# Reciprocal square root of the last three sequences' final layernorm: one GpSimd power, or a Newton iteration on VectorE

## The chip, the cores and the metric

The kernel runs on one core of a Trainium2 chip. A core has five engines that work side by side, each through its own instruction queue in the order in which it was written: TensorE (PE, with its weight loads PEld), VectorE (DVE), ScalarE (ACT), GpSimd (POOL) and SyncE (SP, which here only issues transfers). They wait for each other by semaphores. The metric is the device time of one execution in microseconds (us); a measurement is the median of several executions.

## The reference, cut to what matters

One layer over 16 sequences of 512 tokens with 128 features, all in float32: an attention block with a gate and a layernorm, then a mixture of 8 experts plus a shared expert. After each of the two blocks the sum with its input is normalized:

```python
def _layernorm(x, axis=-1, eps=1e-05):
    m = jnp.mean(x, axis=axis, keepdims=True)
    v = jnp.var(x, axis=axis, keepdims=True)
    return (x - m) / jnp.sqrt(v + eps)
...
    x = L0_attn_x
    x = _layernorm(x + _L0_attn_ref(x, ...), axis=-1)
    x = _layernorm(x + _L0_ffn_ref(x, ...), axis=-1)
    return x
```

In `_L0_ffn_ref` the part that ends last here is the shared expert, `silu(x @ sg) * (x @ su) @ sd` with 1024 hidden features. The kernel adds it to the routed experts' output and to the input, and the second `_layernorm` then gives the result. The change concerns only the `1 / sqrt(v + eps)` of that second layernorm, and of it only the last three of the 16 sequences.

## The kernel before, in words

The 8192 tokens are 64 tiles of 128 tokens (one token to a partition); a sequence is `NC = 4` tiles and there are `NT = 64` tiles. The kernel has two phases. The first does the attention, the first layernorm and the routing; the second does the routed experts and then a closing loop. Work of the shared expert is cut into small steps and kept in a list, `feed`, from which both phases take steps to fill TensorE.

The order of instructions on PE, DVE, ACT and POOL is exactly the order in which Python writes them (`manual_schedule`, no planner). So an instruction that waits holds up everything behind it on its engine.

What the change and its surroundings touch:

- `shared_steps` (the shared expert of one sequence). Eight "gate" steps (`pg`, L125, then ACT's Silu `sl`, L127) alternate with eight "up" steps (`pu`, L133, then DVE's product `h`, L134). Then come eight "down" steps: for each of the sequence's four tiles two halves of the product with `sd` (`pd`, L143), and behind the second half DVE adds the tile's input rows and so empties the accumulator (`x1T<-pd,x`, L148).
- `shared_order` puts the down steps of a sequence behind the first four gate and up steps of the next; the last sequence's down steps have nothing behind them.
- Buffers that bind these steps: three PSUM buffers each for `pg` and `pu` (pool `ps_g`), two for `pd` (pool `ps_d`), two SBUF buffers for `sl`, four for each small tile of the layernorm (pool `small`).
- `finish_lot` (the second layernorm). A lot is a whole sequence (4 tiles) for the first 15 sequences, and a single tile for the four tiles of the last one. For each lot it computes, per tile, the statistics (`st`, L101, and mean and variance `mv`, L103, both DVE), then the reciprocal root by `rstd_of`: DVE adds eps (`ve`, L107), and POOL raises that to the power -0.5 (`rstd`, L109). Then DVE forms `nb = -mean * rstd` (L906), ACT writes `res = rstd * x + nb` for each tile (L909), and SP sends `res` out (L914).
- The closing loop (the `while feed or ends:` at the end of the kernel) takes a step of `feed`, then, once the routed rows are summed, lets `finish_lot` go on to its next `yield`. Two yields lie between `rstd_of` and `nb`, so other DVE work may be written between them while `feed` lasts.

`rstd_of` is used by the first phase also (function `after`, lines 509 and 524); these uses are the same in both kernels.

Of the kernel before, what the change touches and what calls it, by code (L numbers as in the profile page):

```python
# [10 lines left out]
F32 = mybir.dt.float32  # L11
I32 = mybir.dt.int32
AF = mybir.ActivationFunctionType
ALU = mybir.AluOpType
# [5 lines left out]
P = 128  # L20
B, N, D = 16, 512, 128
NC = N // P
T = B * N
NT = T // P
# [5 lines left out]
LN_EPS = 1e-5  # L30
# [17 lines left out]
def tile_kernel(  # L48
# [20 lines left out]
    nc = tc.nc  # L69
# [4 lines left out]
    small = ctx.enter_context(tc.tile_pool(name="small", bufs=4))  # L74
# [23 lines left out]
    def ln_stats(src, mv, n):  # L98
        st = small.tile([P, n, 6], F32, tag="st", name="st")
        for c in range(n):  # L100
            nc.vector.bn_stats(st[:, c, :], src[:, c, :])  # L101
        for c in range(n):
            nc.vector.bn_aggr(mv[:, c, :], st[:, c, :])  # L103

    def rstd_of(var, n, eps):
        ve = small.tile([P, n], F32, tag="ve", name="ve")
        nc.vector.tensor_scalar(ve, var, eps, None, ALU.add)  # L107
        r = small.tile([P, n], F32, tag="rstd", name="rstd")
        nc.gpsimd.tensor_tensor(r, ve, neghalf[:, :n], ALU.pow)  # L109
        return r  # L110


# [64 lines left out]
    with ExitStack() as ph:  # L177
# [317 lines left out]
        def after(b):  # L495
# [11 lines left out]
            mv = small.tile([P, NC, 2], F32, tag="mv", name="mv")  # L507
            ln_stats(o, mv, NC)
            r = rstd_of(mv[:, :, 1], NC, LN_EPS)
            yield  # L510
            w = wk1.tile([P, NC, D], F32, tag="w", name=f"w_{b}")
# [10 lines left out]
            mv2 = small.tile([P, NC, 2], F32, tag="mv2", name="mv2")  # L522
            ln_stats(w, mv2, NC)
            r2 = rstd_of(mv2[:, :, 1], NC, LN_EPS)
            yield
            yield
# [209 lines left out]
        with tc.manual_schedule(engines=ORDERED):  # L736
# [42 lines left out]
            t, over = NT + 1, 12  # L779
# [16 lines left out]
    with ExitStack() as ph:  # L796
# [96 lines left out]
        def finish_lot(lot):  # L893

            n = lot[1] - lot[0]
            mv = small.tile([P, n, 2], F32, tag="mv", name="mv")
            for t in range(*lot):
                while t not in done or t // NC not in summed:
                    yield False
                ln_stats(base[:, t : t + 1, :], mv[:, t - lot[0] : t - lot[0] + 1, :], 1)  # L900
                yield True
            rs = rstd_of(mv[:, :, 1], n, LN_EPS)
            yield True
            yield True
            nb = small.tile([P, n], F32, tag="nb", name="nb")
            nc.vector.scalar_tensor_tensor(nb, mv[:, :, 0], -1.0, rs, ALU.mult, ALU.mult)  # L906
            res = fp.tile([P, n, D], F32, tag="res", name=f"res_{lot[0]}")
            for c in range(n):
                nc.scalar.activation(  # L909
                    res[:, c, :], base[:, lot[0] + c, :], AF.Identity, bias=nb[:, c : c + 1], scale=rs[:, c : c + 1]  # L910
                )
                if c < n - 1:
                    yield True
            nc.sync.dma_start(outv[:, lot[0] : lot[1], :], res)  # L914
            yield True
# [4 lines left out]
        with tc.manual_schedule(engines=ORDERED):  # L920
# [27 lines left out]

            adds = [add_up(b) for b in range(B)]
            ends = [finish_lot(lot) for lot in lots]  # L950
            begun, landed = 0, None

# [72 lines left out]
```

## Time and profile before

| what | value |
|---|---|
| median of 3 runs | 923.22 us (922.89 to 923.61) |
| profiled execution, device time | 925.82 us |
| profiled execution, span from first to last instruction | 924.1 us |
| PE busy | 851.1 us, 92% of the span |
| DVE busy | 557.6 us, 60%, 1687 instructions |
| ACT busy | 442.7 us, 48% |
| POOL busy | 346.7 us, 38%, 461 instructions |
| POOL power, L109, of a 4-tile lot | median of all 51: 1019 ns; in the last sequences 1.01 us |
| POOL power, L109, of a 1-tile lot | 0.54 to 0.55 us, 4 of them |
| last matmul ends | at 910.79 us |
| last ACT instruction starts | at 915.19 us |

Times in the profile are microseconds from the start of the span. A row of the timeline gives the start, the duration, the engine, the line, the operation and the tiles (written `out<-in`), and in brackets the engine's idle time before it with what ended it. An instruction may start before the one ahead of it on its engine has ended, where it doesn't read that one's result: so start-to-start distances, not durations, tell what a chain of instructions takes.

### The profile page before, as it was taken

To read this page: it belongs to the slowest core of one execution; us is meant where nothing else is said; L and a number is where in the kernel's file an instruction comes from. 1 tells how busy PE (TensorE), PEld (TensorE's weight loads), DVE (VectorE), ACT (ScalarE), POOL (GpSimd) and SP (SyncE) were. 2 spreads that over 40 slices of the span, in tenths; PEclk is the share of its full clock that TensorE was granted. 3 is DMA by queue.
4 is the path that set the end of the run, shared out by engine and by line. 5 is a ranking of instruction groups with operands and counts; after the bars stand their busy time and mean duration, and the time that the engine had idled before them with its cause. 6 is when DMAs were issued, how large, how long until landed. Compare 5 with 4: busy or idle time off the path is not lost.

```text
span 924.1 us, 24551 instructions
## 1 busy us (share of the span) xinstructions
PE 851.1 (92%) x9790; PEld 582.2 (63%) x9790; DVE 557.6 (60%) x1687; ACT 442.7 (48%) x1285; POOL 346.7 (38%) x461
## 2 busy tenths in 40 slices
PE   2898999989898898888899999999999999999994
PEld 1666667656765675565555576667777666666663
DVE  6688888976589687778652433333333248854542
ACT  3767677656576665654332233333333324334341
POOL 4022222176733667666656233333333311010100
PEclk9999999999999999999899999999999999999997
DMA  9931111111111111000000522133311035501000
GB/s 279 416 143 32 31 32 31 31 43 57 46 43 34 43 59 50 24 17 9 6 2 2 151 78 64 58 90 87 92 46 37 26 106 171 159 23 35 23 24 23
DMA packets 64339, 62.97 MB, mean 68 GB/s; under 512 B 6179, under 2 KB 55130, under 8 KB 63200
## 3 DMA queue, kind: packets, MB, share of 16 engines
q1 hardware_dynamic: 57392, 50.44, 17.4%
q0 software_dynamic: 6656, 10.69, 3.6%
q8 instruction: 77, 1.26, 0.6%
q14 instruction: 38, 0.31, 0.1%
q10 hardware_dynamic: 176, 0.27, 0.1%
HBM read 32.71 MB, written 31.88 MB: 70 GB/s over the span
## 4 chain that ended last, share of the span: by engine, by line
PE 79%; DVE 13%; issue 3%; ACT 3%; DMA 1%; POOL 0%; POOLq 0%; DVEq 0%; ACTq 0%
PE pd L143 12%; PE pg L125 11%; PE pu L133 10%; PE ped L852 8%; PE peg L936 7%; PE peu L938 7%; PE pe L444 4%; PE pq L363 4%; DVE et L451 3%; PE pout L486 3%; PE pt L399 2%; PE pout L477 2%; PE po L501 1%; PE pout L468 1%; PE pq L366 1%
## 5 line engine op out<-in xcount | busy, mean ns | idle before, releaser
L671 POOL DMA_INDIRECT xg_dram<-x,idx x128 | 134.1, 1048 | 40.3 <-issue 34.4
L109 POOL TENSOR_TENSOR rstd<-ve,neghalf 128x4 f32<-128x4 f32 (+1 forms) x51 | 52.9, 1038 | 250.9 <-DVE ve L107 237.5
L451 DVE TENSOR_TENSOR et<-pe,causal 128x384 f32<-128x384 f32 x256 | 125.0, 548 | 20.4 <-PE pe L444 19.1
L858 POOL DMA_INDIRECT y_dram<-y,to x80 | 77.6, 970 | 153.6 <-ACT y L856 153.6
L941 DVE TENSOR_TENSOR eh<-esl,peu 128x512 f32<-128x512 f32 (+1 forms) x96 | 57.5, 599 | 127.7 <-PE peu L938 125.5
L125 PE MATMUL pg<-x1T,sg_sb 128*128 128x512 f32 x256 | 133.6, 604 | 0.9 <-DVE x1T L148 0.9
L134 DVE TENSOR_TENSOR h<-sl,pu 128x512 f32<-128x512 f32 x128 | 87.7, 685 | 74.5 <-PE pu L133 57.6
L133 PE MATMUL pu<-x1T,su_sb 128*128 128x512 f32 x256 | 131.7, 596 | 0.6 <-DVE h L134 0.3
L127 ACT ACTIVATE sl<-pg 128x512 f32<-128x512 f32 x128 | 76.1, 596 | 111.8 <-PE pg L125 85.8
L143 PEld LDWEIGHTS pd<-sd_sb,h 128*128 128x128 f32 x1024 | 122.9, 197 | 6.7 <-issue 5.5
L143 PE MATMUL pd<-sd_sb,h 128*128 128x128 f32 x1024 | 126.3, 280 | 0.4 <-ACT sl L127 0.4
L852 PEld LDWEIGHTS ped<-rd,eh 128*128 128x128 f32 x640 | 83.9, 192 | 23.7 <-issue 21.8
L936 PE MATMUL peg<-xgT,rg 128*128 128x512 f32 (+1 forms) x192 | 84.6, 522 | 0.0
L938 PE MATMUL peu<-xgT,ru 128*128 128x512 f32 (+1 forms) x192 | 84.4, 521 | 0.0
L852 PE MATMUL ped<-rd,eh 128*128 128x128 f32 x640 | 84.3, 275 | 0.0
L940 ACT ACTIVATE esl<-peg 128x512 f32<-128x512 f32 (+1 forms) x96 | 50.5, 526 | 59.1 <-PE peg L936 49.9
L133 PEld LDWEIGHTS pu<-x1T,su_sb 128*128 128x128 f32 x256 | 45.8, 191 | 46.4 <-issue 40.2
L856 ACT ACTIVATE y<-ped,wt 128x128 f32<-128x128 f32 x80 | 29.4, 368 | 86.8 <-PE ped L852 82.2
L363 PE MATMUL pq<-W,xT 128*128 128x384 f32 x128 | 62.8, 575 | 7.4 <-DVE W L335 6.5
L125 PEld LDWEIGHTS pg<-x1T,sg_sb 128*128 128x128 f32 x256 | 44.9, 193 | 39.0 <-issue 33.7
L486 PE MATMUL pout<-et,vpad 128*32 128x64 f32 x2048 | 50.5, 221 | 13.7 <-issue 13.7
L444 PE MATMUL pe<-q,kT 32*64 32x192 f32 x2048 | 62.1, 338 | 0.0
(165 smaller groups left out, 1285.8 us busy)
## 6 DMA issues: line engine op xcount, KB each, us to landing
y_dram<-zero SPq DMA_DIRECT2D x8, 1024.0 KB, 14.4
y<-y_dram SPq DMA_DIRECT2D x32, 256.0 KB, 3.0
xT<-xt SPq DMA_DIRECT2D x16, 384.0 KB
xg_dram<-empty SPq DMA_DIRECT2D x8, 660.0 KB, 14.6
xg<-xg_dram SPq DMA_DIRECT2D x8, 660.0 KB
x<-x SPq DMA_DIRECT2D x16, 256.0 KB, 2.9
o<-res SPq DMA_DIRECT2D x15, 256.0 KB, 2.3
xg_dram<-x,idx POOLq DMA_INDIRECT x128
```

Source lines behind the costliest of these rows:

```text
L125: nc.tensor.matmul(pg, sg_sb[:, ts(i, P)], seq, start=True, stop=True)
L133: nc.tensor.matmul(pu, su_sb[:, ts(i, P)], seq, start=True, stop=True)
L134: nc.vector.tensor_tensor(h[i // half][:, i % half, :], h.pop(("s", i)), pu, ALU.mult)
L143: nc.tensor.matmul(pd, h[k][:, i - k * half, ts(c, P)], sd_sb[:, i, :], start=(i == 0), stop=(i == IS // P - 1))
L363: nc.tensor.matmul(pq[:, :, 0:24], xts[b][:, c, 0:P], W[:, 0:384].rearrange("p (h n) -> p h n", n=24), start=True, stop=True)
L444: nc.tensor.matmul(pes[g][mine, s], kT[rows, s, mine], q2[rows, s, 3 * i : 3 * i + 3], start=(s == 0), stop=(s == 1),)
L451: nc.vector.tensor_tensor(et.rearrange("p s k n -> p s (k n)"), pes[g].rearrange("p s k n -> p s (k n)"), causal.rearrange("p k n -> p (k ...
L486: nc.tensor.matmul(pout[32 * a : 32 * a + 32, HALF:], vp[:, at : at + 32], et[g][:, s, 1 + j, :], start=False, stop=(gg == 1 and j == 1),)
L671: i = nc.gpsimd.indirect_dma_start(out=xg_dram[:, :], out_offset=bass.IndirectOffsetOnAxis(ap=idx[:, k, t : t + 1], axis=0), in_=x1[:, t, ...
L852: nc.tensor.matmul(pd, h[:, i, ts(c, P)], got[e][2][:, i, :], start=(i == 0), stop=(i == IR // P - 1))
L936: nc.tensor.matmul(pg[:, :n], rg_sb[:, ts(i, P)], xgTs[e][:, ds(o0, n)], start=True, stop=True)
L938: nc.tensor.matmul(pu[:, :n], ru_sb[:, ts(i, P)], xgTs[e][:, ds(o0, n)], start=True, stop=True)
```

## The change: four Newton steps on VectorE

A second way to compute the reciprocal root, `rstd_by_steps`, is added. It adds eps as before, makes a first guess from the bits of the number (shift right by one as an integer, subtract from a constant), and improves it by four Newton steps of three instructions each, `r <- r * (1.5 - 0.5 * ve * r * r)`. All are DVE instructions on a tile of 128 partitions with one element for each tile of the lot. `finish_lot` uses it where the lot starts at tile 52 or later: the two 4-tile lots of sequences 13 and 14, and the four 1-tile lots of sequence 15. All other lots, and the first phase, keep the power on POOL.

```diff
@@ rstd_of (before: L104 to L110) @@
         nc.gpsimd.tensor_tensor(r, ve, neghalf[:, :n], ALU.pow)
+        return r
+
+    def rstd_by_steps(var, n, eps):
+
+        ve = small.tile([P, n], F32, tag="ve", name="ve")
+        nc.vector.tensor_scalar(ve, var, eps, None, ALU.add)
+        guess = small.tile([P, n], I32, tag="guess", name="guess")
+        nc.vector.tensor_scalar(guess, ve.bitcast(I32), 1, None, ALU.arith_shift_right)
+        nc.vector.tensor_scalar(guess, guess, -1.0, float(0x5F3759DF), ALU.mult, ALU.add)
+        r = guess.bitcast(F32)
+        for step in range(4):
+            t = small.tile([P, n], F32, tag="newton", name="newton")
+            nc.vector.tensor_tensor(t, r, r, ALU.mult)
+            nc.vector.scalar_tensor_tensor(t, t, -0.5, ve, ALU.mult, ALU.mult)
+            to = small.tile([P, n], F32, tag="rstd", name="rstd")
+            nc.vector.scalar_tensor_tensor(to, t, 1.5, r, ALU.add, ALU.mult)
+            r = to
         return r
@@ finish_lot @@
-            rs = rstd_of(mv[:, :, 1], n, LN_EPS)
+
+            rs = (rstd_by_steps if lot[0] >= NT - 3 * NC else rstd_of)(mv[:, :, 1], n, LN_EPS)
```

## The prediction

> **What bounds the kernel now.** I read the page first, then the chain of waits of the last 20 us, then the timeline of that stretch, and last the timeline for rows that price a chain of tiny VectorE instructions. The page gives the whole (span, and the group that the change replaces in part):
>
> ```profile
> span 924.1 us, 24551 instructions
> L109 POOL TENSOR_TENSOR rstd<-ve,neghalf 128x4 f32<-128x4 f32 (+1 forms) x51 | 52.9, 1038 | 250.9 <-DVE ve L107 237.5
> ```
>
> POOL is idle before these powers (250.9 us in all, waiting for `ve`): it has nothing else to do. What matters is who waits behind. The chain of waits, in order of time, shows that TensorE carries it without a gap to 910.79 and that behind it stands a serial tail:
>
> ```profile
> 886.18 7.14 PE pd L143 x64
> 893.33 0.86 PE pg L125 x2
> ...
> 903.63 7.16 PE pd L143 x64
> 910.79 0.02 issue
> 910.81 0.29 DVE x1T L148
> ...
> 915.19 0.49 ACT res L909
> ```
>
> Until 903.63 a longer wait on DVE or ACT costs time only if it reaches a TensorE buffer. Of the tail, the timeline shows (start, duration, engine, line):
>
> ```profile
> 906.32 0.15 DVE L107 TENSOR_SCALAR ve<-mv 128x1 f32<-128x1 f32 x1
> 907.24 0.29 DVE L148 TENSOR_TENSOR x1T<-pd,x 128x128 f32<-128x128 f32 x1 [0.76 <-PE pd L143]
> ...
> 911.02 0.14 DVE L107 TENSOR_SCALAR ve<-mv 128x1 f32<-128x1 f32 x1
> 911.33 0.55 POOL L109 TENSOR_TENSOR rstd<-ve,neghalf 128x1 f32<-128x1 f32 x1 [4.13 <-DVE ve L107]
> 911.92 0.16 DVE L906 SCALAR_TENSOR_TENSOR nb<-mv,rstd 128x1 f32<-128x1 f32 x1 [0.76 <-POOL rstd L109]
> 912.00 0.29 DVE L101 BATCH_NORM_STATS2 st<-x1T 128x6 f32<-128x128 f32 x1
> ...
> 912.53 0.15 DVE L107 TENSOR_SCALAR ve<-mv 128x1 f32<-128x1 f32 x1
> ...
> 914.94 0.16 DVE L906 SCALAR_TENSOR_TENSOR nb<-mv,rstd 128x1 f32<-128x1 f32 x1 [0.75 <-POOL rstd L109]
> ```
>
> When TensorE ends, three 1-tile lots (tiles 61, 62, 63) are still to be normalized, one after the other: the statistics of a lot are written behind `nb` of the one before. `ve` to `nb` takes 911.92 - 911.02 = 0.90 us, and 914.94 - 914.04 = 0.90 for the last; from `ve` to the next `ve` is 1.51. So 3 x 0.90 = 2.7 us of the tail are the trip to POOL and back. That is all that the change can gain there, and it holds only if its own instructions cost less.
>
> **The price of a step.** At the start of the kernel there is a chain of instructions on 128x1 tiles, integer ones among them, each reading the one ahead, and one that doesn't:
>
> ```profile
> 2.13 0.15 DVE L238 TENSOR_SCALAR rowi<-rowi 128x1 int32<-128x1 int32 x1
> 2.32 0.15 DVE L240 CAST bitf<-rowi 128x1 f32<-128x1 int32 x1
> 2.50 0.15 DVE L242 TENSOR_SCALAR par<-bitf 128x1 f32<-128x1 f32 x1
> 2.58 0.14 DVE L243 TENSOR_SCALAR par<-bitf 128x1 f32<-128x1 f32 x1
> ```
>
> Dependent instructions start 0.19 and 0.18 apart, that is a duration of 0.15 plus some 0.035; the independent pair starts 0.08 apart. With four columns, line 539 to 541 (453.96, 454.15, 454.35) gives 0.19 and 0.20. `nb`, the scalar-tensor-tensor form that eight of the new instructions have, lasts 0.156 on 128x1, 6 ns more than `ve`. I take 0.187 a step for one column and 0.195 for four. The shift and the integer subtraction aren't in the trace: lower bound 0.08 (the independent pair), upper 0.25 (the 128x4 integer cast at 1.34); over three lots that is -0.6 to +0.4 us. I take 0.187, since line 238 is an integer instruction of the same size.
>
> **Part by part.**
>
> 1. The last three lots. Each loses the trip to POOL (0.90) and gets `ve`, two for the guess and 4 x 3 for the steps, 15 dependent instructions: 15 x 0.187 = 2.81. Each is 1.91 longer, nothing lies beside it, and all three stand in series: 3 x 1.91 = **+5.73 us**.
>
> 2. The lot of tile 60 falls between TensorE's last tiles. Today `ve` starts at 906.32, the power runs on POOL, and meanwhile DVE empties the accumulator of tile 61 at 907.24. In the changed order the 14 new instructions stand ahead of that: the last starts at 906.32 + 14 x 0.187 = 908.94, tile 61 is emptied from 909.02 to 909.31. There are two `pd` buffers, so tile 63's down step needs the one of tile 61. It would have started at 903.63 + 3 x 1.79 = 909.00 and now starts at 909.36 (TensorE followed a release by 0.05 at 14.21); 0.19 more if the first weight load is no longer hidden. So TensorE stalls 0.36 to 0.55; I take **+0.45 us**, all on the path.
>
> 3. Sequence 13's lot (4 tiles). `ve` at 885.72, last step at 885.72 + 14 x 0.195 = 888.45. Behind it wait on DVE the product `h` (888.53 instead of 886.29), `nb` (889.14) and the emptying of tile 56's accumulator (889.22 to 889.51 instead of 888.01). TensorE needs that buffer for the third tile at 886.18 + 3.57 = 889.75. **Zero**, with 0.24 us to spare; without the cover, 14 steps that are 10 ns longer each cost 0.14. The ACT work that waits for `nb` has until 894.29, ACT's next Silu.
>
> 4. Sequence 14's lot. `ve` at 895.76, last step 898.49; `h` of up step 3 ends at 899.26, `nb` 899.18, first `res` 899.37, and queued behind it on ACT is the Silu of gate step 4 (899.77 instead of 898.07). Its `h` ends at 901.08; TensorE needs that `pu` buffer for up step 7 at 902.77. The Silus catch up (901.14, 902.03, and 902.81 as today), and the last `h` starts at 903.74 as today. **Zero**, 1.7 us to spare.
>
> 5. The added waits. The four results of a lot use up the four `rstd` buffers, so the fourth waits for ACT's `res` of the lot before. That one ends 0.74 us after its `nb`, some 2.5 us ahead of need: zero. POOL loses six powers with nothing behind them, and SP's sends are later as their lots are: zero. What follows the last ACT instruction (915.68 to 924.1) is taken as it is.
>
> **Sum**: 5.73 + 0.45 = +6.18 us. The profiled execution took 925.82 (924.1 and 1.7 around the span), 2.6 over the median of the runs; I set the sum on the median: 923.22 + 6.18 = **929.4 us**, and expect a span of some 930.3 in a like profile.
>
> [...] The trace shows a toll that hardly depends on size: 0.15 us for one column, 0.29 for 128. [...]
>
> **Rivals.**
>
> - Not slower: the steps overlap on DVE as the independent pair does, 0.08 apart. Then `ve` to `nb` is 14 x 0.08 + 0.187 = 1.31, the three lots add 3 x 0.41 = 1.2, and item 2 goes: 924.4, within 0.2%. The whole decides at 0.90 / 15 = 0.06 a step, where nothing is lost. Against it: every new instruction reads its predecessor's result, and such pairs stand 0.18 to 0.20 apart in each place I found. 3%.
> - The end isn't set by the last `res`: 8.4 us of the span lie behind it without any engine at work. If something else fixes the end, 6 us could vanish there: 923.2. Against it: the chain of waits ends with that `res`, and its transfer can only follow. 2%.
> - The 4-tile lots stall TensorE too: item 3 has 0.24 us. At 0.21 a step the lots give 6.8, item 2 some 0.8, item 3 a little: 930.9. 5%.
> - Steps as slow as line 540's multiplication at 66.94, 0.44 instead of 0.16 at 454.15. Twelve such a lot would be 2.6 more a lot: over 937. Against it: POOL's addition on line 433 ran at the same moment, and in the last 20 us POOL would be empty. 1%.
> - The switch doesn't reach these lots: it compares the lot's first tile with 52, and in the built kernel's order DVE has 84 instructions more (6 x 14) and POOL six fewer. 1%.
>
> **How the numbers follow.** The forecast holds 88%. Its own ends: at 0.18 a step 5.4 + 0.27, 928.9; at 0.205 a step 6.5 + 0.8, 930.5; the integer instructions move the low end to 928.3, and the runs' own spread is 0.4. The range, 928.0 to 930.8, leaves out the first two rivals, the slow steps and some of the third. A change of 0.2%, 1.85 us, is what a measurement of this kernel can tell from none: slower 0.94 (forecast, stalls, slow steps), same 0.05 (overlap, end not set by the tail), and 0.01 for faster, the last rival's share with room for a gain that I see no case for.
>
> **What would show it.** DVE 1771 instructions, POOL 455; `ve` to `nb` 2.8 us in the last lots with the steps 0.19 apart; a TensorE gap of about half a us ahead of the last tile's down step and none earlier than 903; the same 8.4 us behind the last `res`. I am wrong if steps stand 0.1 apart, if TensorE waits at 889 or 899, or if the stretch behind the last `res` shrinks.

## The result, and the profile after

| | before | changed |
|---|---|---|
| median of 22 executions each | 924.05 us | 925.12 us |
| ratio | 1 | 1.0007 (95%: 0.9994 to 1.002) |
| profiled span | 924.1 us | 923.5 us |

No difference that this measurement can tell; the forecast was +6.2 us. The profile shows the 6.2 us, and where as much was given back. In the changed kernel the lines behind the new `rstd_by_steps` are shifted by 17, and from its call in `finish_lot` on by 18: `ve` is L115, the guess L117 and L118, the steps L122 to L125, `x1T` L165, `pd` L160, `nb` L924, `res` L927; the kernel's closing code, L1021 before, is L1039.

First the chain that ended last, of the changed kernel (start, duration, engine, tile, line):

```profile
901.94 1.80 PE pd L160 x16
...
907.75 2.07 PE pd L160 x16
909.84 0.29 DVE x1T L165
...
920.13 0.17 DVE nb L924
920.38 0.49 ACT res L927
```

From the emptying of the last accumulator to the last `res` it is 920.38 - 909.84 = 10.54 us; before it was 915.19 - 910.81 = 4.38. The tail grew by 6.16 us. Its timeline shows why, for tile 61:

```profile
910.05 0.14 DVE L115 TENSOR_SCALAR ve<-mv 128x1 f32<-128x1 f32 x1
910.22 0.15 DVE L117 TENSOR_SCALAR guess<-ve 128x1 int32<-128x1 int32 x1
910.41 0.15 DVE L118 TENSOR_SCALAR guess<-guess 128x1 int32<-128x1 int32 x1
910.60 0.16 DVE L122 TENSOR_TENSOR newton<-guess 128x1 f32<-128x1 f32 x1
...
912.53 0.16 DVE L123 SCALAR_TENSOR_TENSOR newton<-newton,ve 128x1 f32<-128x1 f32 x1
912.80 0.16 DVE L125 SCALAR_TENSOR_TENSOR rstd<-newton,rstd 128x1 f32<-128x1 f32 x1
912.99 0.16 DVE L924 SCALAR_TENSOR_TENSOR nb<-mv,rstd 128x1 f32<-128x1 f32 x1
913.07 0.28 DVE L101 BATCH_NORM_STATS2 st<-x1T 128x6 f32<-128x128 f32 x1
...
913.61 0.15 DVE L115 TENSOR_SCALAR ve<-mv 128x1 f32<-128x1 f32 x1
```

The steps start 0.19 apart, the integer ones too; only the last one of each of these three lots starts 0.27 behind its predecessor (it waits for ScalarE also, as the last section shows). `ve` to `nb` is 2.94 us where it was 0.90, and a lot takes 3.56 where it took 1.51. TensorE too stalls ahead of the last tile's down step, as these rows of its timeline (weight loads, then matmuls) say in the brackets:

```profile
907.75 1.86 PEld L160 LDWEIGHTS pd<-sd_sb,h 128*128 128x128 f32 x16 [0.64 <-DVE x1T L165]
907.75 2.05 PE L160 MATMUL pd<-sd_sb,h 128*128 128x128 f32 x16 [0.45 <-DVE x1T L165]
```

What gave it back stands behind the last `res`. The rows of the closing code's line list instructions that aren't counted as work: number, durations in ns (least, median, most), first and last start in us. Before:

```profile
L1021 POOLq DRAIN  x3: 40/102/8990, 914.3 to 923.8; - x3
L1021 SPq DRAIN  x3: 7/7/7, 917.4 to 923.6; - x3
L1021 POOLq EVENT_SEMAPHORE_RANGE_CLEAR  x1: 138/138/138, 923.7 to 923.7; - x1
```

After:

```profile
L1039 POOLq DRAIN  x3: 40/102/9455, 875.1 to 923.2; - x3
L1039 SPq DRAIN  x3: 7/7/7, 922.6 to 922.9; - x3
L1039 POOLq EVENT_SEMAPHORE_RANGE_CLEAR  x1: 137/137/137, 923.0 to 923.0; - x1
```

GpSimd's last power, before and after:

```profile
914.37 0.54 POOL L109 TENSOR_TENSOR rstd<-ve,neghalf 128x1 f32<-128x1 f32 x1 [0.97 <-DVE ve L107]
```

```profile
875.14 1.01 POOL L109 TENSOR_TENSOR rstd<-ve,neghalf 128x4 f32<-128x4 f32 x1 [9.03 <-DVE ve L107]
```

At its end each engine here has a drain, an instruction of the closing code that isn't counted as work (the closing line has such rows for all five queues), and in both kernels the end came behind all of them. SP was ready at 917.4 before: the last transfer, issued at 915.7, had landed (a 64 KB `res` took a median of 1.5 us to land). GpSimd wasn't. Its queue began to drain at 914.34, just as its last power started, and the drain lasted 8.99 us, to 923.33, which is 8.42 us behind the end of that power (914.91). Only then did the engines' last instructions follow, from 923.4 on; this meeting of the engines is the rest, 0.78 us. In the changed kernel GpSimd's last power is that of sequence 12, the drain begins at 875.1 and ends 8.42 us behind that power, at 884.57, beside other work. Then SP is the last to be ready, at 922.6, and the span ends 2.58 us behind the last `res` instead of 8.43.

So the change takes 5.85 us off behind the last `res` and puts 6.16 us and the stall ahead of it. Over the stretch from the last matmul to the end the two nearly cancel: 13.66 us after, 13.33 before. That two amounts with separate causes came out so alike is chance.

### The profile page after: what moved, and what is told of

Read it like the earlier page. It is cut to its first block, busy times and chain, and to the rows that moved or that the text cites. A ratio compares the mean times of both kernels' runs of the same rounds, so it can differ in the third digit from the quotient of the medians.

```text
span 923.5 us, 24626 instructions
## 1 busy us (share of the span) xinstructions
PE 847.2 (92%) x9790; PEld 580.0 (63%) x9790; DVE 571.3 (62%) x1771; ACT 442.3 (48%) x1285; POOL 342.7 (37%) x455
## 4 chain that ended last, share of the span: by engine, by line
PE 77%; DVE 15%; issue 4%; ACT 3%; DMA 1%; DVEq 0%; ACTq 0%
PE pd L160 11%; PE pg L142 10%; PE pu L150 10%; PE ped L869 8%; PE peg L954 7%; PE peu L956 7%; PE pe L461 4%; PE pq L380 4%; DVE et L468 4%; PE pout L503 3%; PE pt L416 2%; PE pout L494 2%; PE po L518 1%; PE pq L383 1%; DVE st L101 1%
## 5 line engine op out<-in xcount | busy, mean ns | idle before, releaser
L688 POOL DMA_INDIRECT xg_dram<-x,idx x128 | 134.1, 1048 | 40.2 <-issue 34.5
L109 POOL TENSOR_TENSOR rstd<-ve,neghalf 128x4 f32<-128x4 f32 x45 | 48.8, 1083 | 216.4 <-DVE ve L107 202.2
L160 PE MATMUL pd<-sd_sb,h 128*128 128x128 f32 x1024 | 126.9, 281 | 2.1 <-issue 1.2
L160 PEld LDWEIGHTS pd<-sd_sb,h 128*128 128x128 f32 x1024 | 123.1, 197 | 8.2 <-issue 6.3
```

What stands on the lines that cost most here:

```text
L160: nc.tensor.matmul(pd, h[k][:, i - k * half, ts(c, P)], sd_sb[:, i, :], start=(i == 0), stop=(i == IS // P - 1))
L688: i = nc.gpsimd.indirect_dma_start(out=xg_dram[:, :], out_offset=bass.IndirectOffsetOnAxis(ap=idx[:, k, t : t + 1], axis=0), in_=x1[:, t, ...
```

## The experiments

Two explanations were put against each other. Theory A: the closing drain of GpSimd, 8.42 us behind its last instruction, set the end before, and the change moves it out of the way. Theory B: the stretch behind the last `res` shrank because something counted from TensorE's end fixes the end; both kernels end 13.3 to 13.7 us behind the last matmul. Theory C, where it appears, is the forecast's own assumption that the stretch behind the last `res` is constant. The experiments ran on other chips than the result, where the kernel before takes 888 to 889 us; each ratio is against the kernel before on the same chip. The first half of the kernel varies by some 2 us from one execution to the next: on one chip the same down steps of the middle start at 461.62 in the profile of the changed kernel and at 463.82 in that of the run with one lot and steps, though the two differ only at their end. So the stretch from the last matmul to the end of the span is the sharper number, and the time the confirmation.

**A late instruction on GpSimd.** Both kernels add to the changed one, behind the `rs = ...` line of `finish_lot`:

```diff
+            if lot[0] == NT - 1:
+                late = small.tile([P, n], F32, tag="late", name="late")
+                nc.gpsimd.tensor_tensor(late, mv[:, :, 1], neghalf[:, :n], ALU.pow)   # or ALU.mult
```

> The changed kernel with one more power on GpSimd, on the variance of tile 63 into a tile that nobody reads; all lots keep their Newton steps. Theory A (the closing drain): GpSimd's drain ends 8.42 us after its last power, and the span 0.78 us after the later of this drain and the last output's landing. The power can start some 0.25 us behind mv of tile 63 (7.3 us behind the last matmul) and lasts 0.55, so the span should end 7.6 + 0.55 + 8.42 + 0.78 = 17.3 us behind the last matmul instead of 13.6, and the kernel take 3.7 us more than the changed one. Theory B (the stretch behind the last res is set by something else, counted from TensorE's end): 13.3 to 13.6 us behind the last matmul, no change of time.

> As the run with the late power, but a multiplication in its place. If the long drain follows any GpSimd arithmetic: the span ends some 16.9 us behind the last matmul (the multiplication is 0.2 to 0.55 us) and the kernel takes 3.3 to 3.7 us more than the changed one. If it belongs to the power alone: drain under 1 us, 13.6 us behind the last matmul, no change. Theory B: no change.

Measured behind the last matmul: 17.18 us with the power, 16.82 with the multiplication (0.19 us long). Against the kernel before: 1.005 (1.0033 to 1.0067), that is +4.4 us, and 1.0071 (1.0056 to 1.0085), +6.3 us. Theory A asked for some 0.7 + 3.7 = 4.4 and 4.1; the multiplication's run is 2 us over that, which its profile doesn't show; the two runs' intervals overlap, and I leave it open. The rows of the power's run, GpSimd's timeline and the closing line, and the closing line of the multiplication's:

```profile
883.00 0.55 POOL L923 TENSOR_TENSOR late<-mv,neghalf 128x1 f32<-128x1 f32 x1 [41.07 <-DVE mv L103]
```

```profile
L1042 POOLq DRAIN  x3: 40/102/9007, 883.0 to 892.5; - x3
```

```profile
L1042 POOLq DRAIN  x3: 40/102/8647, 882.8 to 892.0; - x3
```

The drain ends 8.42 us behind the late instruction in both. An instruction on GpSimd whose result nobody reads moves the end, from 13.66 us behind the last matmul in the changed kernel to 17.18 and 16.82; theory B falls, and that the instruction is a power has no part in it.

**The changed kernel with less of a chain, and once more.**

```diff
-        for step in range(4):
+        for step in range(3):
```

> The changed kernel with three Newton steps instead of four. Theory A: in the changed kernel the chain on VectorE sets the end, since the drain is long over; three instructions of 0.193 us less in each of the last three lots are 1.75 us, and TensorE's stall of 0.45 us ahead of the last tile goes: 2.2 us less than the changed kernel, 1.4 less than the kernel before; 11.9 us from the last matmul to the end. Theory B: 13.3 to 13.6 us behind the last matmul, only the 0.45 us of the stall is saved.

> The changed kernel itself, for a price on the same chip as the next three. Theory A: the tail behind the last matmul is 13.66 us (before 13.33) and TensorE stalls 0.45 us ahead of the last tile: 0.8 us over the kernel before. Theory C (the forecast on record: the stretch behind the last res is fixed): 6.2 over.

The shorter one: 11.84 us behind the last matmul, as theory A said; in time 0.9996 (0.9986 to 1.0005), that is -0.4 us with the expected -1.4 just outside the interval's end of -1.2. The changed kernel on another chip: 13.66 us behind the last matmul again, 1.0008 (0.9996 to 1.0021), where theory C wanted 6.2 us. With the drain hidden, the chain on VectorE does set the end. The steps cost about what the forecast said, but more stands against them than the 0.90 us a lot: the drain too.

**Steps for the last two lots alone.**

```diff
-            rs = (rstd_by_steps if lot[0] >= NT - 3 * NC else rstd_of)(mv[:, :, 1], n, LN_EPS)
+            rs = (rstd_by_steps if lot[0] >= NT - 2 else rstd_of)(mv[:, :, 1], n, LN_EPS)
```

> The Newton steps only for the lots of tiles 62 and 63; all others keep the power. Theory A: the last power is that of tile 61, it ends 1.1 us behind the last matmul, its drain with the 0.78 behind it 10.3 us behind the last matmul; the chain of the two lots, each 2.04 us longer, ends with the output's landing 11.6 us behind it. The later of the two, 11.6, is 1.8 us less than the kernel before (13.3). Theory C: two lots of 2.04 more, 4.1 us over the kernel before.

11.69 us behind the last matmul, and 0.9982 (0.9968 to 0.9995), -1.6 us. The closing line:

```profile
L1039 POOLq DRAIN  x3: 40/102/9002, 873.2 to 884.1; - x3
L1039 SPq DRAIN  x3: 7/7/7, 883.5 to 883.8; - x3
```

The long drain ends at 873.17 + 9.00 = 882.17, ahead of SP at 883.5. So moving GpSimd's last power forward by two lots is enough to hide the drain, and the chain is shorter by one lot's steps.

**One lot for tiles 61 to 63.** The edit is against the changed kernel; the second kernel puts `rstd_of` in place of the choice. The `continue` lets the last lot go on in the same pass in which the lot before it ends.

```diff
-        for step in range(4):
+        for step in range(3):
...
-            rs = (rstd_by_steps if lot[0] >= NT - 3 * NC else rstd_of)(mv[:, :, 1], n, LN_EPS)
+            rs = (rstd_by_steps if lot[0] >= NT - 3 else rstd_of)(mv[:, :, 1], n, LN_EPS)
...
-        lots = [(b * NC, b * NC + NC) for b in range(B - 1)] + [(t, t + 1) for t in range(NT - NC, NT)]
+        lots = [(b * NC, b * NC + NC) for b in range(B - 1)] + [(NT - NC, NT - 3), (NT - 3, NT)]
...
                     if went is None:
                         ends.remove(g)
+                        if len(ends) == 1:
+                            continue
```

> Tiles 61, 62 and 63 in one lot, which alone has Newton steps (three); all other lots keep the power, the last of which is that of tile 60, over before the last matmul. Behind the last matmul: the addition of the inputs 0.3, statistics of tile 63 0.5, ve and eleven steps 2.3, nb and ACT's start 0.25, three res 1.3, transfer and end 2.6 to 3.0. Theory A: 7.4 to 7.8 us behind the last matmul, 5.6 us less than the kernel before (0.6%); the drain ends 6 us behind the last matmul and hides. Theory B, counted from TensorE's end: 13.3, no change.

> The same lots as in the run with one lot of three tiles, but with the power on GpSimd for it too. Theory A: the power of three columns starts 1.2 us behind the last matmul and lasts some 0.86; with 8.42 of drain and 0.78 the span ends 11.3 us behind the last matmul, 2.1 us less than the kernel before and 3.6 more than with the Newton steps. Were the drain no matter, this would be the faster of the two by 1.4 us (one trip of 1.2 to GpSimd in place of 12 steps).

With steps: 7.98 us behind the last matmul, a little over the 7.4 to 7.8 expected, and 0.9946 (0.9926 to 0.9967), -4.8 us. With the power: 11.30 us as expected, 0.9969 (0.9957 to 0.998), -2.8 us; the two intervals just overlap. The closing line with steps, then with the power:

```profile
L1041 POOLq DRAIN  x3: 40/102/8995, 870.3 to 882.2; - x3
```

```profile
L1041 POOLq DRAIN  x3: 40/102/9300, 873.9 to 883.7; - x3
```

In the second the last `res` has ended 3.6 us behind the last matmul, in the first 4.7: the power reaches the result 1.1 us earlier, and with its drain the kernel ends 3.3 us later.

**What makes the drain long.** An indirect transfer here writes rows to places that a list of indices gives. The kernel before has 208 of them on GpSimd: 128 scatter rows to the experts (L671, on average 1048 ns of GpSimd each), 80 send the experts' rows home (L858, 970 ns). Three kernels leave some out: all of them, the 80 home, or 40 of these.

```diff
@@ scatter @@
+            return      # no indirect transfers: this and the next
@@ back, ahead of the indirect transfer @@
+            return      # without the rows home
+            if e >= E // 2:    # or: half of the rows home
+                return
```

> The kernel before without any indirect transfer on GpSimd (the rows are neither scattered to the experts nor sent home, so the experts' part of the result is left out; the powers stay where they were). Its time is not of interest, only the drain. [...] Theory B says nothing on the drain and 13.3 us.

> The kernel before without the 80 indirect transfers that send the experts' rows home (the experts' part of the result is left out); the 128 that scatter rows to the experts stay. Only the drain is of interest. If its length goes by the number of indirect transfers: 128/208 of 8.42, 5.2 us. If it is one price for any number: 8.4 us.

> The kernel before with only the 40 indirect transfers home of the first four experts (half of the experts' part of the result is left out); the 128 that scatter are there. Only the drain is of interest: it ended 0.07 us behind the last power without indirect transfers, 1.9 with the 128 and 8.42 with all 208. If each transfer home adds its share: 1.9 + 40 x 0.082 = 5.2 us. If the drain steps up with any transfer home: 8.4; if only with the later ones: 1.9.

| indirect transfers | drain ends behind the last power | from the last matmul to the end |
|---|---|---|
| none | 0.07 us | 7.43 us |
| 128 (scatter) | 1.89 us | 7.50 us |
| 128 + 40 home | 5.16 us | 10.07 us |
| 128 + 80 home (the kernel before) | 8.42 us | 13.33 us |

The powers stood where they were. The rows of the closing line, for none, for 128 and for 168 (each drain begins with the last power, which takes 0.54 of it):

```profile
L1001 POOLq DRAIN  x3: 40/77/641, 878.2 to 881.8; - x3
```

```profile
L1010 POOLq DRAIN  x3: 45/102/2457, 876.4 to 880.0; - x3
```

```profile
L1023 POOLq DRAIN  x3: 40/102/5723, 878.0 to 884.3; - x3
```

So the long drain belongs to the indirect transfers, though in the kernel before the last of them was issued at 746.96, long before the end. The run with the 128 scatters alone fits neither value that was expected of it, 5.2 for a share per transfer and 8.4 for one price: it showed 1.89. From 128 to 208 each transfer home adds 0.082 us ((8.42 - 5.16) / 40 and (5.16 - 1.89) / 40), and with 0.082 the 5.2 us for 168 had been forecast. The first 128 add 0.015 each on average. Whether scatters are cheaper than transfers home, or some hundred transfers are free and all later ones cost 0.082, these runs don't tell.

**The price paid early.** One line in the kernel before, where the last indirect transfer has been written:

```diff
                     if not backs:
+                        nc.gpsimd.drain()
                         for b in range(3):
```

> The kernel before, with one drain of GpSimd's own written behind its last indirect transfer, some 40 us before its next power is wanted; nothing else is changed. If the long drain pays once for the indirect transfers: this early one takes 8.4 us beside other work, the closing one is under 0.1 us behind the last power, and the end follows the last res by 2.6 us: 7.5 us behind the last matmul instead of 13.3, 5.8 us less than the kernel before (0.65%), without any Newton step. If every drain after an indirect transfer is long: 13.3 us, no change.

> Tiles 61 to 63 in one lot, all lots with the power on GpSimd, and the early drain. If the early drain pays for the closing one: the last res ends 3.6 us behind the last matmul as in the run with one lot and the power, and the end follows it by 3.2: 6.8 us behind the last matmul, 6.5 us less than the kernel before (0.7%), and 1.2 less than one lot with Newton steps. If not: 11.3 us, 2.0 less than the kernel before.

The early drain's row and the closing one's, from the run of the kernel before with that line:

```profile
L970 POOLq DRAIN  x1: 9607/9607/9607, 709.6 to 709.6; - x1
```

```profile
L1022 POOLq DRAIN  x3: 34/102/631, 877.3 to 880.9; - x3
```

The early one ends 8.40 us behind the last indirect instruction (which ran from 709.88 for 0.97 us), the closing one 0.07 us behind the last power. GpSimd's next power came at 726.09, so the gap was 15 us, not the 40 of the expectation, and 7 us were to spare. The span ends 7.48 us behind the last matmul, and the kernel takes 0.9924 (0.9909 to 0.9939) of the time before: -6.8 us. With the three tiles in one lot and the power it is 6.83 us behind the last matmul and 0.9927 (0.9915 to 0.994). In time the two can't be told apart. Both beat the kernel before and the changed one, without a Newton step.

## Why the prediction was wrong, point by point

- **The step that failed: "What follows the last ACT instruction (915.68 to 924.1) is taken as it is."** Which engine ends that stretch wasn't asked. GpSimd's drain, counted from the power that the change removes, held up the end by 5.85 of those 8.43 us, and with the change the stretch shrank to 2.58. The late instructions moved the end by their own position, and without indirect transfers the stretch is 2.52 us with all powers in place. The forecast had named this itself as a sign of being wrong.
- **The same error in item 5:** "POOL loses six powers with nothing behind them". Behind the last one stood the drain and the end of the kernel.
- **The rival that held it** ("The end isn't set by the last `res`") had 2% and 923.2 us. Its argument against, that the chain of waits ends with that `res`, was no argument: the chain follows busy instructions, and a drain isn't counted as one. The chain did show the closing code's name: where the last power should stand, a piece is named for POOL's queue and L1021, and the rows of that line hold the 8990 ns.

  ```profile
  914.34 0.58 POOLq L1021
  ```

- **Item 1** was right in its mechanism: +6.16 us for +5.73. A step takes 0.193, not 0.187, and the last step of a lot 0.07 to 0.08 more. That is the wait for ACT's `res` which item 5 had put at zero: it was over in time, and still cost some 0.2 us in the three lots. The price from three small instructions at the start of the kernel held for integer, product and scalar-tensor-tensor forms alike.
- **Item 2** happened at its place. The four down tiles took 7.90 us from the first matmul (901.94 to 909.84) for 7.18 before: 0.72, where I took 0.45 and had 0.55 as the upper bound. The row shows 0.45 of it as idle time; the other 0.27 is that the last tile's 16 matmuls took 2.07 us where the first tile's took 1.80. Their first weight load started only at 907.75, with the matmuls; the forecast had put that at 0.19, and whether it is the whole 0.27 isn't shown.
- **Items 3 and 4** held to 0.11 us: the down steps of sequence 14 took 7.25 us for 7.14, and the up steps behind them ended without a wait.
- **The rival of slow steps** had a wrong sum: twelve steps of 0.44 instead of 0.16 are 3.4 us more a lot, not 2.6. No step was that slow.
- **The price of a small instruction:** the rows here say 0.193 us from start to start in the chain, of which 0.15 to 0.16 is the instruction's own duration. That each instruction reads the one ahead adds some 0.035 on top, as it did at the kernel's start (0.18 to 0.19 apart, at a duration of 0.15).

Summed with what was measured: 6.16 + 0.72 - 5.85 = +1.0 us. The medians differ by 1.07, but the interval of the ratio reaches from -0.6 to +1.8 us, so that so close an agreement is luck.

## What to carry to other kernels

In these kernels an engine's last instruction had a cost that its busy time doesn't show: behind all 208 indirect transfers, and with no drain earlier, GpSimd's closing drain ended 8.42 us behind GpSimd's last instruction, be that at 914.37 (the kernel before), at 875.14 (the changed one) or at 883.00 (with the late power). That was so of GpSimd alone; ScalarE's closing drain, 0.51 us long, ended with its last `res` of 0.49. Where a profile has a stretch of several us behind the last busy instruction, look at the drains of the closing code on each engine before pricing anything at the kernel's end, and count from each engine's own last instruction. Where an engine has issued many indirect transfers, as GpSimd here, a drain placed where the engine is idle can pay that price early; here one line was worth 0.76%, while removing the engine's late work by a slow chain on another engine gained nothing.

## What the runs showed of the hardware that I had not expected

- GpSimd's drain behind 208 indirect transfers ends 8.4 us behind GpSimd's last instruction, 168 us after the last transfer was issued in the kernel before and 131 us in the changed one, whether the last instruction is a power (0.55 us) or a multiplication (0.19 us). It is 0.07 us where there were no transfers, and is paid once: a second drain behind further powers ends 0.07 us behind the last of them. What GpSimd does in this time the profile doesn't show.
- The closing drains of one kernel lie far apart: in the kernel before SP's three took 7 ns each, GpSimd's longest 8990 ns.
- The last Newton step of the last three lots waits for two engines: for VectorE's step before, and for ScalarE's `res` of the lot before, which frees its buffer. It started 0.27 us behind its predecessor (912.53 to 912.80), 0.08 more than a step that waits for VectorE alone, though for tile 61 that `res` had ended at 908.28. Ahead of these three steps, and of no other on that line, VectorE's queue has an instruction that only waits:

  ```profile
  L125 DVEq EVENT_SEMAPHORE  x3: 21/21/21, 912.7 to 919.9; - x3
  ```
